# A four-stage network on one core: the order of the instructions planned on a fuller machine model

## The chip, the cores and the metric

The kernel runs on one core of a Trainium2 chip. The metric is the device time of one execution in microseconds (us); lower is better. A core has engines that work side by side: TensorE (PE) multiplies matrices, with its weight loads shown apart as PEld; VectorE (DVE), ScalarE (ACT) and GpSimd (POOL) work on elements; SyncE (SP) issues DMA transfers. Each engine takes its instructions in the order in which they were put into its queue, and an instruction waits there until what it needs is ready.

## The reference

The input is x, 8 images of 64 channels and 64 x 64 points, in 32-bit floats. Four layers follow each other, each image by itself:

```
layer 0   v = relu(bn(w1 x));  prob = softmax(x^T x / 8) over all 4096 x 4096 pairs of points
          out = prob v;  depthwise 3x3, bn, relu;  1x1, bn;  + x
layer 1   twice (second time shifted by 4): layernorm, attention in 8 x 8 windows, 8 heads,
          projection, + x;  layernorm, MLP 64 -> 128 -> 64 with gelu, + x
layer 2   nine taps, each shifted x * s[tap, point] * cf[tap, channel], summed;
          leaky relu;  a 1 x 9 convolution;  + x
layer 3   layernorm, 64 -> 2 x 128;  depthwise 3x3, silu;  selective scans over the 4096 points
          in 4 directions, 16 states:  h = h * exp(dt * A) + dt * B * u,  y = sum_n C * h
          layernorm, * silu(z), 128 -> 64, + x;  then a pooled depthwise gate, + x
```

The scan is the only recurrence along the points. Layer 2 needs the channel means of a whole image, and the scan of an image needs all of that image's layer 2.

## The kernel before, in words

Two images share the 128 partitions, 64 channels each; there are four such pairs, p = 0 to 3. For a pair, the work has three parts, each written as a Python generator that yields after every piece with an estimated cost:

- `front(p)` (L1260): layer 0 (L1271; scores at L1307, exponentials at L1313, weighted sums at L1299; then the depthwise taps at L1252 and the residual at L1354), layer 1 (`window_head` L1379, `window_row` L1420 with the matmuls L1435 and L1462, `mlp` L1516), layer 2 (L1538; a tap is a matmul L1570, a product on DVE L1573 and a summing matmul L1574; the 1 x 9 convolution is L1584, the residual L1587), and `scan_sources` (L1592), which writes the scan's inputs xc, xt and z to DRAM for both images of the pair, one after the other.
- `scans(p)` (L1657): per image 4 directions x 8 chunks of 512 points are 32 units; a unit has 8 steps of two states. That is 512 steps for a pair and 2048 in all. A step has a product on POOL (`products`, L1731, vd = B * du), two exponentials on ACT (L1753), two scans on DVE (L1756), small copies of the end states (L1764), the multiplication by C on POOL (L1767, L1771) or DVE (L1771, L1776, L1777), and the summing matmuls on PE (L1795). B and C come from DRAM, repeated to all partitions, 512 KB each (L1726, on SP); there are three buffers each for B and C, and six for vd. `inputs` (L1697) prepares a unit: it loads a chunk of xc or xt, and writes the rows of B and C.
- `back(p)` (L1814): the end of layer 3.

A field `dense`, set while layer 0's attention is being written down, gives more of the multiplications by C to DVE and fewer to POOL in the steps that are written meanwhile.

`begin` (L1178) writes down front(0), and beside it layer 0 of pair 1. Then, for each pair, `scans` writes the steps down with the other work between them: back(p - 1), and the front of p + 1 (without layer 0 for p = 0, where it is already done). This is the pace:

```
                while done < cost * (i + 1) / (n - LEAD):
                    done += next(beside, cost)
```

So the work beside the scans is spread evenly over the 512 steps of a round, and is all written down 24 steps before its end. The first scan of round p + 1 needs `scan_sources` of that pair.

What is written down is the program order, not yet the order of the queues. The tile framework has a scheduler that plays the program on a model of the machine when the context closes: of the instructions that the model finds ready for an engine, it takes the one that was written first, and puts it into that engine's queue; buffers are given out at the same time. The order of each queue is thus set by when the model takes instructions to be ready. A few orders are fixed by hand: `behind` (L442) ties the first summing matmul of a step to the multiplication of the next (L1795), and `log_exp` (L436) ties loads of ACT's function table to the instruction ahead of them. Other loads of a function table are put in where two neighbours in ACT's queue need different tables. The numbers of scan steps that run between one piece of a front and the next are therefore a result of the model, not of the text.

After the four rounds a check of ranges decides whether a general path runs (L1939); with these inputs it doesn't.

## Time and profile before

| | |
|---|---|
| median of 3 runs | 13439.18 us |
| lowest and highest | 13437.7 and 13443.52 us |
| span of the profiled execution (its own time) | 13435.7 us |
| first scan starts | 2192 us |
| rounds of 512 steps, p = 0, 1, 2, 3 | 2566, 3213, 3203, 2261 us |
| busy over the span: PE, DVE, ACT, POOL | 80%, 66%, 53%, 58% |
| ACT table loads at L438 | 77 of 1283 ns |

The span runs from the first instruction of the profiled execution to its last, and no other time is given for it. The rounds are cut where the DVE queue takes the first scan of steps 0, 512, 1024 and 1536; the last one includes the end of pair 3's back part. A busy share is the time in which an engine works on something; an engine that is not busy waits for a semaphore, for a buffer or for its sequencer. PE's instructions overlap, so its busy time is the time in which at least one is under way.

### The profile page before, as it was taken

To read this page: it belongs to the slowest core of one execution; us is meant where nothing else is said; L and a number is where in the kernel's file an instruction comes from. 1 tells how busy PE (TensorE), PEld (TensorE's weight loads), DVE (VectorE), ACT (ScalarE), POOL (GpSimd) and SP (SyncE) were. 2 spreads that over 40 slices of the span, in tenths; PEclk is the share of its full clock that TensorE was granted. 3 is DMA by queue.
4 is the path that set the end of the run, shared out by engine and by line. 5 is a ranking of instruction groups with operands and counts; after the bars stand their busy time and mean duration, and the time that the engine had idled before them with its cause. 6 is when DMAs were issued, how large, how long until landed. Compare 5 with 4: busy or idle time off the path is not lost. (4 is left out here: it accounts for less than half of the span.)

```text
span 13435.7 us, 140355 instructions
## 1 busy us (share of the span) xinstructions
PE 10771.7 (80%) x45762; PEld 3974.5 (30%) x45762; DVE 8806.3 (66%) x10407; ACT 7082.9 (53%) x15569; POOL 7764.7 (58%) x3875
## 2 busy tenths in 40 slices
PE   9999986888787669989888666997898766666676
PEld 2243322333232222224433222223443222222222
DVE  0121236777768676676666767667676767987987
ACT  5556514565535646655554644664654554454553
POOL 0000004888778765466666686446766677787883
PEclk9999977998898789989899788998989878888888
DMA  0000004666667765455555675445545577677884
GB/s 24 1 1 1 1 14 166 233 236 218 212 213 239 237 206 170 161 182 173 172 177 175 224 241 177 157 161 179 192 170 170 195 239 260 233 281 263 293 297 156
DMA packets 706250, 2385.13 MB, mean 178 GB/s; under 512 B 81120, under 2 KB 81248, under 8 KB 704480
## 3 DMA queue, kind: packets, MB, share of 16 engines
q1 hardware_dynamic: 681312, 2319.76, 51.0%
q10 hardware_dynamic: 24192, 56.29, 1.1%
q8 instruction: 362, 5.93, 0.2%
q14 instruction: 384, 3.15, 0.1%
HBM read 2272.97 MB, written 102.76 MB: 177 GB/s over the span
## 5 line engine op out<-in xcount | busy, mean ns | idle before, releaser
L1731 POOL TENSOR_TENSOR vd<-B,du 128x1024 f32<-128x1024 f32 x2048 | 4832.8, 2367 | 3958.5 <-DMA B<-rows 2538.2
L1795 PE MATMUL yd<-vd,pack 128*128 128x512 f32 x7540 | 4300.3, 701 | 1351.0 <-POOL vd L1767 585.1
L1753 ACT ACTIVATE dad<-du,As 128x512 f32<-128x512 f32 x4096 | 2729.4, 681 | 1136.3 <-DVE hd L1756 686.4
L1756 DVE TENSOR_TENSOR_SCAN hd<-dad,carry,vd 128x512 f32<-128x512 f32 x2166 | 2714.5, 1270 | 683.9 <-ACT dad L1753 392.9
L1795 PEld LDWEIGHTS yd<-vd,pack 128*128 128x128 f32 x7540 | 1509.5, 217 | 3824.9 <-issue 1678.9
L1767 POOL TENSOR_TENSOR vd<-hd,C 128x1024 f32<-128x1024 f32 x658 | 1551.0, 2357 | 1050.5 <-DVE hd L1756 690.5
L1756 DVE TENSOR_TENSOR_SCAN dad<-dad,carry,vd 128x512 f32<-128x512 f32 x1418 | 1791.8, 1275 | 118.9 <-ACT dad L1753 64.8
L1771 POOL TENSOR_TENSOR vd<-hd,C 128x512 f32<-128x512 f32 x1154 | 1477.9, 1281 | 522.0 <-DVE hd L1756 474.3
L1313 ACT ACTIVATE e<-s 128x512 f32<-128x512 f32 x2048 | 1200.8, 591 | 750.3 <-PE s L1307 748.7
L1307 PE MATMUL s<-X 64*128 64x512 f32 x4096 | 1343.9, 646 | 30.5 <-ACT e L1313 28.8
L1299 PE MATMUL po<-e,VT 128*64 128x512 f32 x4096 | 1227.0, 621 | 12.6 <-ACT e L1313 9.9
L1771 DVE TENSOR_TENSOR vd<-dad,C 128x512 f32<-128x512 f32 x1300 | 866.0, 673 | 67.1 <-ACT carry L1764 46.8
L1764 ACT ACTIVATE carry<-hd 128x1 f32<-128x1 f32 (+1 forms) x1586 | 316.8, 201 | 908.0 <-DVE hd L1756 904.9
L1764 ACT ACTIVATE carry<-dad 128x1 f32<-128x1 f32 x1422 | 240.5, 169 | 786.5 <-DVE dad L1756 783.6
L1307 PEld LDWEIGHTS s<-X 64*128 64x128 f32 x4096 | 375.6, 186 | 914.9 <-issue 782.8
L1447 DVE TENSOR_TENSOR w_e<-w_s,bias 128x512 f32<-128x512 f32 x512 | 330.0, 681 | 426.9 <-PE w_s L1435 426.3
L1462 PEld LDWEIGHTS w_av<-vals,w_e 64*64 64x64 f32 x16384 | 538.9, 143 | 195.4 <-issue 84.2
L1462 PE MATMUL w_av<-vals,w_e 64*64 64x9 f32 x16384 | 567.1, 206 | 32.0 <-ACT w_e L1452 31.8
L1706 PE MATMUL pdd<-xs,xdt 128*128 128x512 f32 x512 | 343.0, 757 | 236.8 <-DMA xs<-xc 102.8
L1452 ACT ACTIVATE w_e<-w_e 128x512 f32<-128x512 f32 x512 | 311.9, 626 | 367.7 <-DVE w_e L1447 250.6
L1299 PEld LDWEIGHTS po<-e,VT 128*64 128x64 f32 x4096 | 236.3, 135 | 847.2 <-issue 763.6
L1574 PE MATMUL acc<-tap,pack 128*128 128x512 f32 x576 | 367.1, 761 | 98.2 <-DVE tap L1573 96.8
(252 smaller groups left out, 11102.0 us busy)
## 6 DMA issues: line engine op xcount, KB each, us to landing
B<-rows SPq DMA_DIRECT2D x2048, 512.0 KB, 5.1
C<-rows SPq DMA_DIRECT2D x2048, 512.0 KB, 4.5
xs<-xt SPq DMA_DIRECT2D x128, 256.0 KB, 3.6
xs<-xc SPq DMA_DIRECT2D x128, 256.0 KB, 4.2
xc<-xcv ACTq DMA_DIRECT2D x64, 256.0 KB, 3.9
zs<-z ACTq DMA_DIRECT2D x64, 256.0 KB, 3.8
xt<-XT ACTq DMA_DIRECT2D x32, 512.0 KB, 7.9
rows<-bc SPq DMA_DIRECT2D x256, 64.0 KB, 1.6
```

The lines of the kernel that those rows point to most:

```text
L1299: nc.tensor.matmul(po[half[im]], lhsT=VT[:, t, half[im]], rhs=es[im], start=(t == 0), stop=(t == 31))
L1307: nc.tensor.matmul(ss[im], lhsT=at(half[im], t), rhs=X[half[im], jc * CH : (jc + 1) * CH], start=True, stop=True)
L1313: nc.scalar.activation(e, ss[im], AF.Exp, scale=C**-0.5, accum_out=parts[:, im, t, jc : jc + 1])
L1462: nc.tensor.matmul(self.av[half[im], x % 4 + j, h, :], lhsT=es[h // 4][half[im], j, h % 4, :], rhs=V[half[im], x + j, h, :], start=True, s ...
L1574: nc.tensor.matmul(acc, lhsT=w["ident"], rhs=tap, start=(t == 0), stop=(t == TAPS - 1))
L1731: self.nc.gpsimd.tensor_tensor(v, st["B"], dx.to_broadcast([P, 2, TD]), ALU.mult)
L1753: nc.scalar.activation(da, u["du"][:, 0], AF.Exp, scale=net.As[:, k, n : n + 1])
L1756: nc.vector.tensor_tensor_scan(along(to), along(da), along(v[:, j]), first, ALU.mult, ALU.add)
L1764: nc.scalar.activation(cs, ends, AF.Copy)
L1767: st["w"] = nc.gpsimd.tensor_tensor(v, h, CC, ALU.mult)
L1771: m = engine.tensor_tensor(v[:, j], hs[j], CC[:, j], ALU.mult)
L1795: m = nc.tensor.matmul(u["y"], lhsT=w["ident"], rhs=v, start=start, stop=stop)
```

## The change

One argument of the context that the program is written into. With it, the scheduler plays the program on the fuller machine model, in which each queue and each DMA engine is modelled apart; without it, on a plain one. The text of the kernel, and so the program order, the tiles, the buffers' numbers and the pace of `scans`, stay as they are.

```diff
     out = nc.dram_tensor("out_0", (B, C, HH, WW), F32, kind="ExternalOutput").ap()
-    with tile.TileContext(nc) as tc:
+    with tile.TileContext(nc, schedule_with_timeline_sim=True) as tc:
         tile_kernel(tc, ax, aps, layout, out)
```

The built program has the same matmuls, element instructions and DMAs; of table loads on ACT in the path that runs it has 439 instead of 370. The orders of all five queues differ.

## The prediction

> **What bounds the kernel now.** First the page, for the span and its regimes.
>
> ```profile
> span 13435.7 us, 140355 instructions
> ...
> PE   9999986888787669989888666997898766666676
> ...
> DVE  0121236777768676676666767667676767987987
> ...
> POOL 0000004888778765466666686446766677787883
> ```
>
> No engine is full throughout. For six slices of 336 us PE works alone; then PE, DVE and POOL share the load. Next, the time windows of the opening, cut where the tap, window and attention lines begin and end, and of the four rounds of 512 scan steps (one per image pair):
>
> ```profile
> 127.00:601.00 474.00, 474.00 (x1797) 116.46 (x1796) 6.42 (x10) 283.45 (x896) 0.00 (x0) 1.00 0.00 1
> 1690.00:2005.00 315.00, 277.19 (x514) 91.81 (x513) 104.16 (x168) 39.25 (x61) 0.00 (x0) 0.73 0.03 13
> 2009.00:2192.00 183.00, 79.97 (x109) 24.04 (x110) 106.27 (x169) 81.22 (x117) 3.02 (x2) 0.61 0.25 95
> 718.00:1688.00 970.00, 951.31 (x8154) 386.99 (x8154) 216.84 (x427) 563.91 (x1332) 0.00 (x0) 0.98 0.01 2
> ...
> 2192.00:4758.00 2566.00, 2007.78 (x9142) 811.58 (x9140) 1871.69 (x2091) 1380.90 (x2681) 2099.63 (x1025) 0.88 0.68 228
> 4758.00:7971.00 3213.00, 2634.93 (x11310) 985.34 (x11310) 2235.66 (x2635) 1773.42 (x3886) 1991.95 (x971) 0.88 0.55 186
> 7971.00:11174.00 3203.00, 2613.25 (x11282) 973.70 (x11282) 2235.54 (x2625) 1759.14 (x3864) 1995.03 (x971) 0.89 0.55 185
> 11174.00:13435.00 2261.00, 1507.36 (x2618) 499.84 (x2618) 1950.25 (x2141) 1080.21 (x2422) 1673.18 (x895) 0.85 0.74 256
> ```
>
> Columns after the length: busy PE, PEld, DVE, ACT, POOL; granted clock; DMA share; GB/s. Seven attention columns alone take 474 us: PE-bound. From 718 to 1688 the windows and MLPs of pair 0 run under the attention of pair 1, PE 98% busy. Layer 2 nearly alone costs 315 us, the scan sources 183 us. The costliest groups show the scan's own work:
>
> ```profile
> L1731 POOL TENSOR_TENSOR vd<-B,du 128x1024 f32<-128x1024 f32 x2048 | 4832.8, 2367 | 3958.5 <-DMA B<-rows 2538.2
> L1756 DVE TENSOR_TENSOR_SCAN hd<-dad,carry,vd 128x512 f32<-128x512 f32 x2166 | 2714.5, 1270 | 683.9 <-ACT dad L1753 392.9
> ```
>
> (busy us, mean ns | idle before, what ended it), and the waits (us in total, times, longest):
>
> ```profile
> POOL vd L1731 <- PE yd L1795: 769.3, 181, 19.0
> POOL vd L1767 <- DVE hd L1756: 690.5, 179, 23.5
> ```
>
> Of the 2538 us for B, 2172 is the one first wait; B costs at most 366 us later. A step costs 5.0 us in round 0 (2566/512), near POOL's 4.1 (2100/512).
>
> **The Trainium skill.** "Perfetto Trace Analysis", Optimization Strategy, says that a kernel with several regimes can gain from interleaving them. The trace agrees: layer 2 of pair 2 lies at 6990 to 7323 us beside 40 scan steps (333 us, of which 40 x 5.0 = 200 is scan), so beside scans it costs 133 us, alone 315. "ScalarE: Activation LUTs", What ACT_TABLE_LOAD costs: 1283 ns, plus 1380 ns of drain; the trace has 1283 ns for each of the 77 loads at L438; the drain isn't shown. "TensorE: Matmul & The Clock Gate", What's actually happening, says that an idle PE is throttled: the granted clock above is 1.00 in dense attention and 0.61 in the sources.
>
> **What the change moves.** Every compute instruction and DMA stays, apart from ACT table loads (370 become 439). I placed each instruction of both programs by the last scan step ahead of it on its engine; durations come from this trace, PE's by what each line adds to PE's busy union. The program order (priority) is unchanged, so what moves is what the new model finds ready later.
>
> 1. *Opening.* Both attentions are now interleaved from the start and end together; behind them stand both convolutions, then pair 0's windows and MLPs, uncovered. Attention: 474/7 = 67.7 us a column, x16 = 1083, plus 100 for start and values: 1185. Then 170: on DVE 16 chunks x (nine taps at 0.74 + 1.28) = 128, and about 40 of normalisation. The 16 window rows and 16 MLP chunks: PE alone needs 434. A row is 22.5 us on PE; I add 4.5 for its tail (normalise, transpose, project), where nothing else fills the waits: 27. An MLP chunk is 5.9 us on ACT with two table loads, about 13 as a chain: 9.5. So 16 x 27 + 16 x 9.5 = 584; ends 434 and 800. Of the added table loads 34 fall here (two sets alternate in each normalisation): 34 x 1.28 = 44, partly inside the estimate. Layer 2 315, sources 183. Sum 1185 + 170 + 584 + 498 = 2437, against 2192: **+245**.
>
> 2. *Rounds 1 and 2.* Pair 2's front falls behind: its attention ends at step 804 instead of 681, and all of its layer 2 stands behind the last scan of the round (it was at steps 865 to 905). So do 3.25 window rows and 8 MLP chunks, and the first image's sources (100 of the 183). Round 2 ends likewise with 8 rows, 13 MLPs, layer 2 and sources for pair 3. The next round's first scan reads those sources, so nothing covers these tails: 3.25 x 27 + 8 x 9.5 + 315 + 100 = **579**; 8 x 27 + 13 x 9.5 + 315 + 100 = **755**. PE's load alone, 394 and 524, is the lower end; rows of 40 and chunks of 14 us the upper: 657 and 917.
>
> 3. *What the scans win back.* I cut the rounds into 64 bins of 32 steps and took each bin's most loaded engine. Before, these sum to 10066 us and took 11244: ratio 1.117 (by round 1.148, 1.124, 1.118, 1.073; a tenth of the bins is below 0.99, a tenth above 1.26). After, without the tails, they sum to 9308; x1.117 = **10397**, so 847 us are saved, mostly because bins with attention fall from 209 (PE) to about 152 (DVE, whose own multiplications are more there).
>
> 4. *Fine order.* On SP, the C fetch mostly stands three steps behind its B instead of one (round 0: 297 of 512 at three, before 331 at one); POOL's multiplications stand 2.8 products behind their scan (before 2.3). C lands in 4.5 us, under one step of 5.0, and DVE's multiplications at L1771 waited 16.7 us for it in all. Covered while POOL stays two products ahead; if that cover goes at a quarter of the 1300 DVE multiplications, by 1.5 us, that is 488, as much as the upper ratio below adds. The other sign: of POOL's waits for yd (769) and DVE (690 and 474) a later multiplication could spare some. I take 0; ratios 1.04 to 1.17 give 9680 to 10890. Loads of source stages slip into round 3: 82 extra table loads there, 105 us on ACT, whose bins (at most 143) stay under DVE's (144 to 190), so hidden; if not, 105. SP's other loads and stores keep within a few steps of their fetch, or move with their stage; queued ahead of a fetch, a load of the back part would hold B.
>
> Sum: 2437 + 10397 + 579 + 755 = 14168 against the span of 13436 (2192 + 11244); the runs' median, 13439, is 3 us higher. I say **14150**, +5.3%.
>
> **Rivals.**
> - *The scans pack tightly (faster).* The finer model of queues may leave fewer stalls within the bins. For it: before, round 3 ran at 1.073; POOL's waits for yd and DVE could go. Against: leads of ACT over DVE are unchanged (0.27 steps both). Only the ratio changes: (13436 - 3771)/9308 = 1.038 is the break-even; at 1.02 the time is 9494 + 3771 = 13265.
> - *Serial parts cost only PE's load.* Good pipelining of windows and layer 2: 2287 + 394 + 524 + 10397 = 13602. Against: layer 2 alone left PE idle for 38 of 315 us at clock 0.73.
> - *Serial parts are latency chains.* Rows of 40, chunks of 14: 864 instead of 584, tails 657 and 917: 2717 + 1574 + 10397 = 14688. For it: the sources at 183 us with no engine above 58%.
> - *No difference.* All five queues are reordered, the opening wholly; only a cancellation gives it.
>
> **How the numbers follow.** Chances: my forecast 0.60 (own range 13780 to 14480), latency chains 0.16, PE's load 0.13, tight scans 0.08, none 0.03. The range, 13600 to 14600, leaves out the faster cases and the worst chains, about 0.2. A measurement tells 0.2% from no change: faster 0.08, same 0.03, slower 0.89.
>
> **What would show it.** Right: the first scan at 2300 to 2650 us; two gaps of 400 to 900 us with POOL idle, holding every layer-2 tap of the round; scan steps of 4.7 to 5.3 us before each gap. Wrong: POOL busy through the round ends, or B and C waits of hundreds of us on POOL or DVE. It fails first on the window rows' uncovered pace, then on the ratio.

## The result, and the profile after

The changed kernel takes 14298.65 us (median of 4 runs, 14289.23 to 14303.09), against 13438.44 us for the kernel before (4 runs, 13408.89 to 13443.52): a ratio of 1.0635, 95% interval 1.0615 to 1.0654. It is slower by about 860 us. The forecast was 14150 us, with 13600 to 14600 as the range.

The page of the changed kernel, for the span and its slices:

```profile
span 14297.6 us, 140592 instructions
...
PE   9998788688898669999888865899978885666666
...
DVE  0002322587778778956876269965686227897987
...
POOL 0000000398888877687885045587886004587883
```

A slice is now 357 us. POOL, which does nothing but scan work, starts one slice later, and there are two holes in its row, at slice 23 and at slices 32 and 33. The holes are the tails of rounds 1 and 2. Between them POOL stands at 5 to 8 where it stood at 4 to 7 before.

The time windows of the changed kernel, with the columns of the prediction's windows (length; busy PE, PEld, DVE, ACT, POOL; granted clock; DMA share; GB/s). In order: fourteen of the sixteen attention columns, the windows and MLPs of pair 0, layer 2, the sources, round 0, and the two stretches without a scan:

```profile
264.00:1368.00 1104.00, 1103.54 (x3667) 272.20 (x3666) 23.90 (x39) 568.48 (x1766) 0.00 (x0) 1.00 0.00 1
1519.00:2266.00 747.00, 602.56 (x6178) 350.15 (x6178) 181.80 (x375) 296.29 (x421) 0.00 (x0) 0.65 0.00 1
2287.00:2561.00 274.00, 262.32 (x456) 84.24 (x456) 68.72 (x106) 28.26 (x43) 0.00 (x0) 0.79 0.02 7
2564.00:2745.00 181.00, 78.93 (x110) 25.16 (x110) 105.68 (x167) 81.69 (x118) 2.38 (x2) 0.61 0.26 95
2745.00:5200.00 2455.00, 2018.88 (x9218) 826.92 (x9218) 1896.50 (x2122) 1417.05 (x2739) 2104.12 (x1025) 0.90 0.71 240
7767.00:8366.00 599.00, 477.19 (x1964) 185.75 (x1962) 189.73 (x328) 173.65 (x256) 6.17 (x5) 0.75 0.06 20
11030.00:11857.00 827.00, 668.89 (x3769) 297.66 (x3767) 243.25 (x437) 257.54 (x376) 5.77 (x3) 0.71 0.04 15
```

The first scan starts at 2745 us instead of 2192. From the last scan of a round to the first of the next it is 596 and 824 us, where it was 18 and 15. In both stretches POOL does next to nothing. The groups of the first one say what is done there:

```profile
L1573 DVE SCALAR_TENSOR_TENSOR tap<-XP,cf,pb 128x512 f32<-128x512 f32 x72 | 52.4, 746 | 104.6 <-PE pb L1570 104.6
...
L1462 PE MATMUL w_av<-vals,w_e 64*64 64x9 f32 x896 | 38.8, 225 | 2.1 <-ACT w_e L1452 2.1
...
L1534 PE MATMUL pf<-hid,pack 128*64 128x512 f32 x32 | 21.9, 816 | 5.9 <-ACT hid L1529 5.9
```

All 72 tap products of the pair (9 taps x 8 chunks) are in the hole; so are 896 of 4096 records of L1462, 3.5 of 16 window rows, and 8 MLP chunks (4 records each). In the second hole the same groups have 72, 2048 (8 rows) and 52 (13 chunks).

The four rounds, from first scan to first scan, take 2455, 3166, 3491 and 2440 us. Against the kernel before, the span goes up by 862 us:

| part | before, us | after, us | difference |
|---|---|---|---|
| opening, to the first scan | 2192 | 2745 | +553 |
| gaps behind rounds 1 and 2 | 33 | 1420 | +1387 |
| scan rounds without the gaps | 11211 | 10132 | -1079 |
| span | 13436 | 14298 | +862 |

The third line is a sum of different signs: rounds 0, 1 and 2 are 111, 625 and 521 us shorter without their gaps, and round 3 is 179 us longer (2261 before, 2440 after).

The groups and waits of the changed kernel show the third line at work. The scan's own instructions have kept their durations:

```profile
L1731 POOL TENSOR_TENSOR vd<-B,du 128x1024 f32<-128x1024 f32 x2048 | 4833.3, 2370 | 5213.7 <-DMA B<-rows 4377.5
L1756 DVE TENSOR_TENSOR_SCAN hd<-dad,carry,vd 128x512 f32<-128x512 f32 x2166 | 2701.4, 1271 | 648.4 <-ACT dad L1753 484.8
```

and two of POOL's waits on PE and DVE have gone down, from 769.3 and 690.5 us, while a third, which was 474.3 us, has gone up (us in total, times, longest):

```profile
POOL vd L1731 <- DMA B<-rows: 4377.5, 149, 2726.1
POOL vd L1771 <- DVE hd L1756: 590.6, 225, 10.8
POOL vd L1731 <- PE yd L1795: 373.7, 156, 13.5
POOL vd L1767 <- DVE hd L1756: 348.6, 147, 8.7
```

Of the 4377.5 us that POOL waited for B, three single waits make up 4140: 2726.1 for the first scan, 592.5 and 821.1 in the two holes. The other 238 us are spread over the rounds, and for these the kernel before had at most 366. So POOL isn't held by late fetches but by the serial work ahead of each round's first B. DVE's waits for C at L1771, 16.7 us before, are 150.1 us here, in 137 waits of at most 6.5.

### The profile page after: what moved, and what is told of

It reads as the page before. It is cut to its first block, busy times and chain, and to the rows that moved or that the text cites. A ratio compares the mean times of both kernels' runs of the same rounds, so it can differ in the third digit from the quotient of the medians.

```text
span 14297.6 us, 140592 instructions
## 1 busy us (share of the span) xinstructions
PE 11664.1 (82%) x45762; PEld 4298.2 (30%) x45762; DVE 8808.5 (62%) x10407; ACT 7197.7 (50%) x15638; POOL 7763.3 (54%) x3875
## 5 line engine op out<-in xcount | busy, mean ns | idle before, releaser
L1731 POOL TENSOR_TENSOR vd<-B,du 128x1024 f32<-128x1024 f32 x2048 | 4833.3, 2370 | 5213.7 <-DMA B<-rows 4377.5
L1795 PE MATMUL yd<-vd,pack 128*128 128x512 f32 x7540 | 4103.7, 678 | 874.6 <-POOL vd L1771 302.7
L1767 POOL TENSOR_TENSOR vd<-hd,C 128x1024 f32<-128x1024 f32 x658 | 1553.0, 2360 | 532.4 <-DVE hd L1756 348.6
L1771 POOL TENSOR_TENSOR vd<-hd,C 128x512 f32<-128x512 f32 x1154 | 1475.9, 1280 | 642.8 <-DVE hd L1756 590.6
L1307 PE MATMUL s<-X 64*128 64x512 f32 x4096 | 1600.9, 645 | 8.7 <-ACT e L1313 8.5
L1299 PE MATMUL po<-e,VT 128*64 128x512 f32 x4096 | 1489.2, 620 | 8.2 <-ACT carry L1764 5.8
L1771 DVE TENSOR_TENSOR vd<-dad,C 128x512 f32<-128x512 f32 x1300 | 876.3, 682 | 345.2 <-ACT carry L1764 184.4
L1307 PEld LDWEIGHTS s<-X 64*128 64x128 f32 x4096 | 429.7, 186 | 1136.5 <-issue 884.8
L1462 PEld LDWEIGHTS w_av<-vals,w_e 64*64 64x64 f32 x16384 | 670.3, 169 | 291.8 <-issue 171.6
L1462 PE MATMUL w_av<-vals,w_e 64*64 64x9 f32 x16384 | 705.6, 222 | 58.5 <-ACT w_e L1452 58.3
L1299 PEld LDWEIGHTS po<-e,VT 128*64 128x64 f32 x4096 | 271.5, 135 | 1060.6 <-issue 854.3
L1240 PE MATMUL pv<-n_sq,pack 128*128 128x512 f32 x576 | 361.8, 714 | 143.4 <-ACT n_sq L1238 142.1
```

The lines of the kernel that those rows point to most:

```text
L1240: nc.tensor.matmul(pv, lhsT=avg, rhs=sq, start=True, stop=True)
L1299: nc.tensor.matmul(po[half[im]], lhsT=VT[:, t, half[im]], rhs=es[im], start=(t == 0), stop=(t == 31))
L1307: nc.tensor.matmul(ss[im], lhsT=at(half[im], t), rhs=X[half[im], jc * CH : (jc + 1) * CH], start=True, stop=True)
L1462: nc.tensor.matmul(self.av[half[im], x % 4 + j, h, :], lhsT=es[h // 4][half[im], j, h % 4, :], rhs=V[half[im], x + j, h, :], start=True, s ...
L1731: self.nc.gpsimd.tensor_tensor(v, st["B"], dx.to_broadcast([P, 2, TD]), ALU.mult)
L1767: st["w"] = nc.gpsimd.tensor_tensor(v, h, CC, ALU.mult)
```

## The experiments

Each run keeps the whole computation. Orders are changed by ties like the kernel's own `behind`, and the scheduler plays the program anew around each tie; so other orders can move with it, and each run's opening, rounds and gaps are read from its own profile. Ratios are to the kernel before, run beside it on the same chip.

| run | starts from | median, us | ratio, 95% interval | opening | rounds | gaps |
|---|---|---|---|---|---|---|
| pairs in turn | after | 13913.39 | 1.0329 (1.0312 to 1.0347) | 2366 | 2438, 3155, 3488, 2469 | 572, 821 |
| table set | after | 14266.70 | 1.0591 (1.0572 to 1.0611) | 2721 | | 605, 822 |
| twins | after | 14059.17 | 1.0449 (1.0426 to 1.0472) | 2539 | 2540, 3143, 3405, 2451 | 630, 828 |
| paced | after | 14358.62 | 1.0657 (1.0639 to 1.0676) | 2754 | 2451, 3408, 3420, 2331 | 13, 13 |
| three without pace | after | 13671.52 | 1.0163 (1.0146 to 1.0180) | 2216 | 2522, 3111, 3386, 2437 | 633, 820 |
| all four | after | 13806.73 | 1.0268 (1.0237 to 1.0298) | 2197 | 2515, 3387, 3386, 2313 | 12, 11 |
| pairs broken | before | 13993.06 | 1.0371 (1.0314 to 1.0429) | 2795 | 2572, 3221, 3196, 2282 | |
| bare tails | before | 13811.46 | 1.0277 (1.0254 to 1.0301) | 2197 | 2565, 3311, 3375, 2358 | 424, 422 |
| POOL lag | before | 14058.28 | 1.0451 (1.0428 to 1.0475) | | 2759, 3282, 3250, 2567 | |
| DVE order | before | 13392.87 | 0.9951 (0.9934 to 0.9967) | | 2552, 3195, 3174, 2284 | |
| C later | before | 13471.05 | 1.0009 (1.0000 to 1.0018) | | 2552, 3221, 3206, 2313 | |
| C later and DVE order | before | 13393.72 | 0.9954 (0.9941 to 0.9968) | | 2488, 3196, 3178, 2330 | |

### The opening: pairs in turn, table set

Pair 1's first value matmul is tied behind pair 0's last weighted sum on PE:

```diff
+                if p == 1 and g == 0:
+                    net.behind(m, net.last_po)
```

> The changed kernel with one more order on PE: the first value matmul of pair 1 stands behind the last weighted sum of pair 0, so the two attentions of the opening follow each other. If the opening lost its time because the two attentions were merged and left pair 0's windows bare, the first scan comes at 2200 to 2350 us instead of 2745, the windows of pair 0 take over 900 us again but under the attention, and the time is about 13780 (13700 to 13900). If the windows are bare whatever the attention does, the first scan stays at 2650 to 2800 and the time at 14200 to 14300. The rounds keep their uncovered tails (about 600 and 830 us) in either case.

The opening falls by 379 us, to 2366, a little above what was expected; rounds and gaps stay within 29 us of the changed kernel's. The time window in which pair 0's windows and MLPs now run under pair 1's attention:

```profile
769.00:1880.00 1111.00, 1089.60 (x8082) 415.10 (x8080) 234.91 (x452) 581.58 (x1313) 0.00 (x0) 0.93 0.01 2
```

PE is 98% busy, as it was in the kernel before (970 us, 951 busy). So the larger part of the opening's loss is the merging of the two attentions, which leaves pair 0's windows with nothing beside them. That the stretch is still 141 us longer than before is for the most part the matter of the twins, below: in the run that restores them and the table set too, it takes 981 us.

In the second run a load of ACT's table set for logarithm and exponential is tied behind the square roots of the preparation, in place of one that is free to move:

```diff
+        self.log_exp(self.last_sqrt)
...
-        net.log_exp()
```

> The changed kernel with the load of the logarithm-and-exponential table tied behind the square roots, where it stood before: 35 table loads fewer, 32 of them in the bare windows of the opening. If a load is on the chain of each window row with its own 1283 ns, the opening is 41 to 45 us shorter and the time about 14255. If the row's other waits hide it, under 10 us. If the drain of 1380 ns that the Trainium skill gives comes on top, about 90 us.

The loads go from 439 to 404, and the opening from 2745 to 2721. So 24 us come back, between the two that were expected. Where they come from is not where the expectation looked. Of the 34 added loads only 16 stand among the windows; 18 stand in the normalisation ahead of the first window. The time window of that normalisation, of the changed kernel and of this run:

```profile
1469.00:1520.00 51.00, 25.88 (x33) 8.14 (x33) 12.97 (x18) 45.13 (x54) 0.00 (x0) 0.66 0.10 41
1471.00:1500.00 29.00, 17.57 (x36) 5.71 (x34) 13.57 (x20) 23.38 (x38) 0.00 (x0) 0.99 0.17 72
```

It is 22 us shorter, and 17 of the loads lie inside it (one just ahead): 17 x 1.283 = 21.8. So where ACT is busy for 45 of 51 us, the whole load counts. The windows and MLPs behind it take 742 us instead of 746: nearly all of their 16 loads is hidden. In the changed kernel's trace ACT's next instruction mostly starts 0.01 to 0.02 us after a load's end, so no drain is seen either.

### The opening: pairs broken, twins

A column of attention took 474/7 = 67.7 us before; in the changed kernel fourteen columns take 1104 us, 78.9 each, at the same granted clock of 1.00 and with PE busy throughout. The two images of a pair lie on two halves of the partitions. A score's matmul (L1307) contracts over 64 rows, a weighted sum (L1299) fills 64 columns; call the two matmuls that the two images have of the same step of such work twins, and adjacent where one stands right after the other in PE's queue. In the kernel before, 256 of pair 0's 256 score twins are adjacent in the queue; in the changed one 155, 162, 140 and 127 of 256 in the four pairs. To price this alone, the kernel before was given the order score, sum, score, sum for pair 0, so that 8 of its 256 stay adjacent:

```diff
+                        if m is not None:
+                            net.behind(n, m)
...
+                        if last is not None and p == 0:
+                            m = weigh(*last, (im,))
+                            net.behind(m, n)
```

> The kernel before, with pair 0's attention alone ordered so that no score matmul stands next to its twin of the other image (score, sum, score, sum in place of two scores, two sums): 8 of 256 twins adjacent instead of 256. If adjacency sets the price, the changed kernel's column (79.5 us with 62 percent of twins adjacent, against 67.7 us) gives 11.8 / 0.38 = 31 us a column more: a column of about 98 us, the end of pair 0's attention about 240 us later, time about 13680. If adjacency is of no account and the longer column came from the merging itself (two streams sharing ACT and the banks), the column stays within 70 us and the time within 13400 to 13480.

The mechanism is right, its price twice what was expected. PE's timeline (start, us, line, operation, records; a matmul in this type leaves two records) of the kernel before:

```profile
301.73 1.13 PE L1307 MATMUL s<-X 64*128 64x512 f32 x4
302.78 1.08 PE L1299 MATMUL po<-e,VT 128*64 128x512 f32 x4
```

and of the kernel with broken pairs:

```profile
800.12 1.12 PE L1309 MATMUL s<-X 64*128 64x512 f32 x2
801.17 1.07 PE L1299 MATMUL po<-e,VT 128*64 128x512 f32 x2
```

Two twins take 1.13 us together; one of them takes 1.12 us alone. The Trainium skill, "TensorE: Matmul & The Clock Gate", Part 3 (packing small matmuls), says that matmuls that use less than 128 rows or columns can run at the same time on different tiles of the array. The trace agrees, and adds that here only neighbours in the queue on different halves did. Seven columns, in a time window of this run:

```profile
304.00:1209.00 905.00, 905.00 (x1793) 214.96 (x1792) 5.54 (x8) 306.49 (x896) 0.00 (x0) 1.00 0.00 0
```

905/7 = 129.3 us a column, 1.91 times 67.7. PE "busy" for 100% of both stretches says nothing of the half of the array that stands idle. The opening rises by 603 us and the rounds don't move, since only pair 0's attention was touched. Eight columns at this price give 493 us of the 603. About 100 more are the first 200 us, in which PE works through the first column at half the granted clock, though it is just as busy:

```profile
100.00:200.00 100.00, 100.00 (x103) 20.05 (x103) 0.00 (x0) 17.87 (x52) 0.00 (x0) 0.50 0.00 0
```

(At 129.3 us for 256 records, these 103 would take 52 us; up to 304 us it is the same.) Of the four executions two took about 13920 us and two, one of them traced, about 14065; whether the two shorter ones lack this stretch is not shown.

The traces also tell why the price was underrated. What seems to count is not whether a matmul has its own twin beside it, but whether it has any partner on the other half. Counted as records of L1307 and L1299 that start within 0.06 us of another one, 96% run in company in the seven columns of the kernel before, 3% in this run, and 79% in the fourteen columns of the changed kernel, more than the 62% of its own twins that are adjacent there. A straight line from 67.7 us at 96% to 129.3 at 3% gives 78.9 at 79%, which is what the changed kernel took.

The other way round, in the changed kernel a twin's first score was held, in the scheduler's plan, until the exponential that frees the second one's bank:

```diff
+                        if free is not None and im == 0:
+                            net.behind(s, free)
...
+                        free = free or a
```

> The changed kernel with the first score matmul of a pair held until the exponential has run that frees the bank of its twin, so that the twins come up together: 248, 248, 189 and 193 of 256 are adjacent by image pair, in place of 155, 162, 140 and 127. If broken twins cost the opening its longer columns, a column goes from 79.5 to 68 to 71 us, the opening is 130 to 170 us shorter and the time 14080 to 14180. If two merged streams are slower for another reason, the column stays at 78 to 81 and the time within 14250 to 14330.

Now 248, 248, 189 and 193 of 256 are adjacent, and fourteen columns take, in a time window of this run,

```profile
213.00:1156.00 943.00, 943.00 (x3582) 234.28 (x3582) 11.25 (x17) 566.23 (x1788) 0.00 (x0) 1.00 0.00 1
```

67.4 us each, the old price, with 97% of the records in company. The opening falls by 206 us, more than was expected. The rounds add up to 13 us less, with round 0 being 85 us longer and round 2 86 us shorter.

### The tails: bare tails, paced

First the question of what cover for a tail is worth, in the old order. In the kernel before, the first layer-2 matmul of pairs 2 and 3 is held behind the last summing matmul of the round:

```diff
+        if p in (1, 2):
+            self.net.behind(self.held, self.net.last_y)
```

> The kernel before, with one order on PE for pairs 2 and 3: the first matmul of layer 2 stands behind the last summing matmul of the round, so layer 2 and the first image's sources run bare at the end of rounds 1 and 2, and all else keeps the order of before. In the trace of before the six stretches with layer 2 and the sources took 1156 us against 6 x 150 without a front: about 256 us for layer 2 and both images' sources; some 200 of them would become a bare stretch of about 400. If cover is worth what the prediction said, two gaps of about 400 us appear and the time rises by about 400 to 13840 (13700 to 14000). If cover is worth little, as the paced run seems to say, the time stays within 13440 to 13600.

The two stretches without a scan, in time windows of this run:

```profile
7551.00:7975.00 424.00, 346.10 (x612) 112.97 (x611) 145.09 (x187) 89.85 (x160) 96.53 (x48) 0.80 0.18 65
10926.00:11348.00 422.00, 343.13 (x607) 112.39 (x607) 145.74 (x187) 88.04 (x158) 97.90 (x49) 0.80 0.19 66
```

The gaps grow by 846 - 33 = 813 us, and the rounds without them fall from 11211 to 2565 + (3311 - 424) + (3375 - 422) + 2358 = 10763, so 448 us are won back where layer 2 no longer stands beside scans. Net it is 362 us by the medians (370 by the profiles): in the old order a bare tail costs nearly half of its length.

Then the reverse, in the changed kernel: the summing matmul of a step may not stand ahead of the front matmul that was written 16 steps earlier, so that PE's queue can't leave the front behind.

```diff
+            if mark is not None and j == 0:
+                net.behind(m, mark)
```

> The changed kernel with the front held to the scans on PE: the first summing matmul of a step stands behind the newest front matmul that was written down 16 steps earlier. Layer 2 of pairs 2 and 3 then lies at steps 873 to 922 and 1385 to 1434 again. If the tails are lost cover, both gaps without scans vanish, rounds 1 and 2 have their loads of 2847 us each in place of 2761 and 2970 with tails, which at the changed kernel's ratio of about 1.09 to 1.12 takes 3100 to 3190 each (3166 and 3491 without the pacing), and the time is 13720 to 13900; the opening stays at 2745. If the cover is worth nothing on the chip, because the stretches beside scans grow by as much, the time stays at 14200 to 14400.

The tie does what it should: layer 2 stands at steps 873 to 922 and 1385 to 1434, and the gaps are 13 us. But the time doesn't fall (1.0657 of the kernel before, against 1.0635). Rounds 1 and 2, in time windows of this run:

```profile
5205.00:8613.00 3408.00, 2812.39 (x11282) 1052.14 (x11282) 2244.84 (x2624) 1767.98 (x3865) 2002.21 (x971) 0.86 0.52 174
8613.00:12033.00 3420.00, 2831.43 (x11282) 1060.88 (x11282) 2251.70 (x2624) 1771.34 (x3867) 2001.96 (x971) 0.86 0.52 174
```

Together 6828 us, against 3166 + 3491 = 6657 with the holes; round 3 is 109 us shorter. So the tails are not won back by this tie, as the rival had it. But the tie has a price of its own. POOL's waits for PE at its product, 373.7 us in all without it, are

```profile
POOL vd L1733 <- PE yd L1797: 1454.9, 323, 43.9
```

A summing matmul that must stand behind the front on PE also stands behind what the front waits for, which would explain them. So the run doesn't show that a covered tail is worth nothing in the new order, only that this way to cover it isn't worth it; no other way was run.

### Together: three without pace, all four

The three ties of the opening (turn, table set, twins) on the changed kernel, without the pace and with it:

> The changed kernel with three of the four repairs, without the pacing: attentions in turn, the table set, twins together (249, 230, 193 and 187 of 256); layer 2 of pairs 2 and 3 lies bare at the ends of the rounds again. The opening is 2190 to 2230 us. If pacing is worth nothing in the new order, rounds 1 and 2 take about 3140 and 3400 as in the twins run and the time is 13650 to 13780, below the run with all four (13807). If the pacing saves with the twins repaired, the time is 13850 to 13950.

> The changed kernel with all four repairs: attentions in turn, the table set, the front paced to the scans, and the twins together (249, 230, 230 and 231 of 256). From the paced run, 14359, the attentions in turn take 379 and the table set 32; if broken twins are also what kept the paced rounds long, the attention there goes from 757 to about 660 us in each of two rounds: 13700 to 13780. If the twins don't matter in the rounds, 13900 to 13960. If the paced rounds are long because every front piece waits worse in the new order, windows and layer 2 stay at 1.2 times their time of before (window stretch near 900 us) in both cases.

The opening is restored in both: 2216 and 2197 us, against 2192. The time window of it in the run without the pace has PE busy 2053 us, where the changed kernel has 2373:

```profile
0.00:2216.00 2216.00, 2053.24 (x11412) 714.12 (x11412) 517.09 (x917) 1091.80 (x2716) 4.20 (x16) 0.91 0.04 14
```

That accounts for the 553 us of the opening by undoing them: 379, 206 and 24 one by one, 529 together, as they overlap. The pace, on top, makes the time longer by some 135 us (13671.52 to 13806.73, between the two ranges that were expected), and so it has no value here either. What the paced front costs shows in one stretch, the windows and MLPs of pair 2 beside the scans of round 1. Time windows of that stretch, of the run with all four:

```profile
6063.00:7132.00 1069.00, 877.41 (x6811) 442.09 (x6812) 596.39 (x764) 534.88 (x978) 578.82 (x281) 0.79 0.43 145
```

and of the kernel before:

```profile
6098.00:6961.00 863.00, 767.92 (x6807) 380.69 (x6808) 592.13 (x759) 507.27 (x953) 576.87 (x281) 0.90 0.54 181
```

The same work (the counts and the busy times of DVE and POOL agree within 1%) takes 206 us more. PE is busy 109 us more and idle 97 us more. Busy time by clock is 877.41 x 0.79 = 693 and 767.92 x 0.90 = 691, so the busy part is the same work at a lower clock. POOL's waits for PE at its product grow by as much as 270 us there, first the kernel before, then the run with all four:

```profile
POOL vd L1731 <- PE yd L1795: 67.1, 13, 11.0
POOL vd L1739 <- PE yd L1803: 336.9, 49, 39.0
```

In the whole run with all four they are 1425.3 us, in the one without the pace 342.4. That fits the tie as the cause; which came first, these waits, PE's idle time or the clock, no run separates.

What stays of the loss in the run without the pace is 236 us of span: opening +24, gaps +1420, rounds without the gaps -1208.

### The rounds: POOL lag, DVE order, C later

Round 0 has no front with layer 0 in it and no tail, and it went from 2566 to 2455 us. Busy POOL stays (2100 and 2104 us), so it is 115 us of POOL's idle time. Three features like those of the new order were put into the kernel before, one by one: POOL's multiplication three to four products behind (2.8 on average in the new order), DVE's multiplication by C ahead of the next step's scans, and the C fetch two steps later on SP (mostly three in the new order).

```diff
+                if i >= 1 and "pool" in steps[i - 1]:
+                    self.net.behind(steps[i - 1]["pool"], steps[i + 2]["p"])
```

> The kernel before, with POOL's multiplications by C held behind the product of three steps later (3 to 4 steps behind their scan everywhere; before it was 1 in a third of round 0 and most of round 3). If that lag is what made round 0 quicker in the changed kernel (2455 us against 2566 with the same loads), round 0 takes 2450 to 2490, rounds 1 and 2 lose 20 to 80 each, and the time is about 13250 (13150 to 13350), faster than before. If the lag is of no account, round 0 stays at 2540 to 2590 and the time within 13400 to 13480.

```diff
+            if st.get("ahead") is not None:
+                net.behind(s, st["ahead"])
```

> The kernel before, with DVE's multiplication by C held ahead of the next step's scans (in round 0 all 256 right after their own scan; before 104 of 256, in the changed kernel 234). An early multiplication lets the summing matmul, and with it POOL's next product, come earlier. If that is what made round 0 quicker in the changed kernel (2455 us against 2566), round 0 takes 2440 to 2500, rounds 1 and 2 lose 20 to 60 each, round 3 up to 40, and the time is 13200 to 13350. If it is not, round 0 stays at 2540 to 2590 and the time within 13400 to 13500.

```diff
+                if i + 3 - 2 >= 0:
+                    self.net.behind(steps[i + 3 - 2]["dmaC"], steps[i + 3]["dmaB"])
```

> The kernel before, with each C fetch on SP held behind the B fetch of two steps later (427 of 512 in round 0 at two; before 331 at one; in the changed kernel 297 at three). In round 0 POOL is the fullest engine (2099 of 2565 us before, 2103 of 2454 after), and its waits for B fell from 127 to 26 us. If B waited in SP's queue behind C fetches whose buffers were not yet free, round 0 takes 2450 to 2500 and the time is 13250 to 13370. If the place of C is of no account, round 0 stays at 2540 to 2590 and the time within 13400 to 13490. If C then comes too late for the multiplications, as holding POOL's multiplications back cost 4.5 percent, the time is over 13550.

> Both orders on the kernel before: C two steps behind B on SP, and DVE's multiplications ahead of the next step's scans (which alone gave 0.9951). If the two gains add, 13180 to 13310, the fastest of all; if C's place is of no account, 13370 to 13420; if C comes too late, over 13500, and more than in the run without the DVE order, since DVE now waits for C at once.

The lag alone is bad: round 0 takes 2759 us, and in this run's waits POOL is held by B:

```profile
POOL vd L1733 <- DMA B<-rows: 1170.7, 639, 14.4
```

None of these 639 waits is longer than 14.4 us, so the opening is not in the sum; the kernel before had at most 366 us of such waits. That a buffer of B comes free later when the multiplications stand further behind is the likely cause, and wasn't tested apart. DVE's order, in all 256 of its multiplications of round 0 instead of 104, leaves round 0 at 2552, so it isn't what made that round quicker. It is worth 0.5% of the whole all the same, 13392.87 against 13448.86 us, and with that faster than both kernels. C later changes nothing (1.0009), nor does it add to DVE's order (0.9954 and 0.9951); the 2488 us of round 0 in that last run come from one profile, and its total doesn't confirm a gain. What made round 0 quicker in the new order is left open: none of the three alone, nor this one pair, gives it.

## Why the prediction was right, and where its steps were not

The direction, the range and the mechanism held: a longer opening, two bare tails, and rounds that win back part. The span is some 130 us above the sum of 14168, and this is made of three errors of different sign: opening +308, tails +86, scans -265. That the number came so near is in part luck: without the scans' error it would have been about 14560, just inside the range.

**Opening: +245 forecast, +553 measured.** The order was as forecast (both attentions together, convolutions, then bare windows). By parts, measured against the step's terms: attention to 1368 us against 1185; convolutions and normalisation 151 against 170; windows and MLPs 747 against 584; layer 2 274 against 315; sources 181 against 183; and gaps of 24. Two terms failed.
- *"474/7 = 67.7 us a column, x16".* The duration was taken from an order in which twins are adjacent, and the new order parts 101 and 94 of 256 in the two pairs of the opening, which leaves 79% of the matmuls a partner instead of 96%. A column costs 78.9 us; for the fourteen measured ones that is 156 us of the 183. The runs with broken and with restored twins (129.3 and 67.4 us) show the cause. PE's busy time was treated as a property of the instructions, and it is one of their order.
- *"A row is 22.5 us on PE; I add 4.5".* The first eight rows take 1519 to 1810 us, 36.4 each; a chunk of MLP about 10.3 against 9.5. It isn't the added waits that were mis-sized: 747 - 603 = 144 us of PE idle, where 584 - 434 = 150 had been allowed. PE's own load is 603 us instead of 434, and the granted clock there is 0.65 (a mean over the stretch), where the kernel before has 0.98 in the stretch with the same pieces; 603 x 0.65 = 392 and 434 x 0.98 = 425, so the clock is enough to explain the rise. The same 32 full matmuls of a row's start, in the kernel before (718 to 1688 us) and in the bare windows (1519 to 2266), show it in their own durations, 644 and 1137 ns:

```profile
L1396 PE MATMUL w_q<-w_h,pack 128*128 128x512 f32 x32 | 18.0, 644 | 0.2 <-DVE w_h L1392 0.2
L1396 PE MATMUL w_q<-w_h,pack 128*128 128x512 f32 x32 | 33.1, 1137 | 45.9 <-DVE w_h L1392 45.9
```

The prediction named the page that says that an idle PE is throttled (the Trainium skill, "TensorE: Matmul & The Clock Gate", What's actually happening), saw 0.61 in the sources, and didn't apply it to the windows, which it made sparse itself. Rows near 40 are what the rival of latency chains had; its chunks of 14 were too dear. The rows' pace was named in the prediction as the first thing to fail.
- The 34 added table loads were put at 44 us, partly inside. The run with the table set gives 24, nearly all from the 18 loads of the normalisation ahead of the windows.

**Tails: 579 and 755 forecast, 596 and 824 measured.** The right pieces are in them: 3.5 rows (3.25 forecast), 8 chunks and the 72 taps; 8 rows, 13 chunks and 72 taps. The second is low by 69 us, and it is the one with more rows; at the 36.4 us of the opening its eight rows alone would add 75. Layer 2, 274 us in the opening instead of 315, would take 41 off again. These are estimates, as the pieces of the tail weren't timed apart; what is left of the 69 us stays open.

**Scans: 10397 forecast, 10132 measured.** The scans won back 11244 - 10132 = 1112 us instead of 847. The ratio of 1.117 that was carried over was too high: it is 10132/9308 = 1.0885, inside the 1.04 to 1.17 that was allowed. POOL's waits for PE at L1731 and for DVE at L1767 fell by 396 and 342 us, which is the thing that the rival of tight scans named, and those for DVE at L1771 rose by 116; that rival needed 1.038 and didn't get there. The steps of rounds 0, 1 and 2 take 2455/512 = 4.8, (7767 - 5200)/512 = 5.0 and (11030 - 8366)/512 = 5.2 us, inside the 4.7 to 5.3 that were to be seen.

**Fine order, taken as nothing.** For C it was right as far as it was run: two steps later gives 1.0009. Three steps were not run alone, and in the new order DVE waits 133 us more for C. POOL's lag costs 4.5% at three to four products; what the 2.8 of the new order are worth was not run. The 82 loads of round 3 weren't taken out alone. Round 3 took 179 us more, with 117 loads instead of 35. In the paced runs, with 24 loads, it took 2331 and 2313 us, and in the old order with bare tails, with 36, 2358; but in all of these other work moved too, so the share of the loads stays open.

**Beyond the time.** That bare tails are a loss in themselves is shown for the old order (+362 us for 846 bare). In the new one the only cover that was tried gained nothing, with a tie that costs something itself. The prediction's sum doesn't say this, since it counted tails and scans apart; a reader would have taken from it that the 1334 us of tails are there to be had. Of the extra 860 us the three ties take back 637, by the medians against the kernel before beside each, and the opening's share is 529 in the profiles. What is left, 223 us by the medians, is bare tails less what the scans win back, and no run here removed it.

## What to carry to other kernels

Take an engine's busy time from another order only where the neighbours in its queue stay the same: here matmuls on half of the array overlapped with the other half's only as neighbours, and the bare stretches ran at a granted clock of 0.61 to 0.79. So price a stretch that becomes bare as PE's load, times the old clock over the clock seen in a sparse stretch, plus its waits. Before covering a hole, measure what the work costs beside the scans in that very order, and what the tie that puts it there makes others wait: what is won by the cover can be lost again in the pace of both. And price a table load by its place: at its full length where its engine is the one that is full, at little where the chain waits elsewhere.

## What was not expected of the hardware

- Two half-array matmuls of 512 columns in 32-bit floats take 1.13 us as neighbours on different halves, and 1.12 us each otherwise; a column (32 twins of scores and 32 of sums) takes 67.4 to 67.7 us where 96 to 97% of the records start together with another, 78.9 at 79%, and 129.3 at 3%. Busy time shows 100% in all three.
- The granted clock was 0.65 in bare windows with PE busy for 81% of the time (602.56 of 747 us), lower than the 0.79 of layer 2 at 96% (262.32 of 274). In the run with broken pairs it was 0.50 for the first 200 us with PE busy throughout, and 1.00 behind them with the same work. So the busy share alone doesn't tell the clock; what sets it wasn't tested.
- 17 table loads of 1283 ns in a normalisation with ACT busy for 45 of 51 us cost 22 us, their full length; 16 in the bare windows cost about 4 us.
